# Layer 0: when GpSimd masks the adjacency tiles of x's side and of the late table

## The chip, the cores and the metric

The kernel runs on one core of a Trainium2 chip. The metric is the device time of the program in microseconds; the median of three runs before is 3467.49 us (3466.55 to 3467.74).

## The reference

Four graph layers run one after the other on x (64 x 256 x 256) with adjacency matrices adj (64 x 256 x 256), each with a residual sum and a layer norm. The change concerns layer 0, a recurrence over the 256 nodes: step i replaces row i of h, and later steps read it.

```python
d = jnp.sum(adj, axis=-1)
dinv = jnp.where(d != 0, 1.0 / jnp.where(d != 0, d, 1.0), 0.0)
norm_adjT = jnp.swapaxes(adj, 1, 2) * dinv[:, :, None]
def step(h, i):
    x = jnp.take(h_e, i, axis=1)
    row = jnp.take(norm_adjT, i, axis=1)
    x_par = jnp.einsum('bj,bjd->bd', row, h)
    iou = x @ W_ioux.T + b_ioux + x_par @ W_iouh.T + b_iouh
    r, z = jnp.split(iou, 2, axis=1)
    r, z = (jax.nn.sigmoid(r), jax.nn.sigmoid(z))
    hc = jnp.tanh(x @ W_coux.T + b_coux + x_par * r @ W_couh.T + b_couh)
    h_new = z * x_par + (1.0 - z) * hc
    return (jax.lax.dynamic_update_slice(h, h_new[:, None, :], (0, i, 0)), None)
h_out, _ = jax.lax.scan(step, h_e, jnp.arange(n))
```

x_par of node i is thus a sum over nodes not yet replaced (their h is still x) and over nodes already replaced (their h is new).

## The kernel before

Layer 0 is the loop over `now` in `_recurrence`, one turn for each node; the other layers follow. The order of the instructions on every engine is written out by hand (`manual_schedule`). Steps are grouped in parts of U = 8 and blocks of T = 32. Below, p is a step's place in its part (0 to 7), i its place in its block (0 to 31), k the block.

The sum x_par is gathered in tiles `ACC`, one for each part, from these sources:

- **x's side**: nodes that are not yet replaced. For the first 128 nodes it is computed before the loop; for the last 128 nodes the generator `x_side` (from L317) does it inside the loop, in sixteen tiles of XB = 4 batch entries. A tile is loaded in two transfers (`xA` from adj, `xX` from x; three buffers each), its `xA` is masked with a triangle by `cut` (L332, a multiplication on GpSimd, called POOL in the profile), and then four products run on PE (L212), one for each turn of the generator. Its results go through PSUM, ACT and DRAM (`Us`) into `ACC`.
- **near and far**: each new state is added to the next nodes at once, on DVE (`push`, L628) for the nearest, and on POOL (`push_far`, L661 and L665) for the rest of this part and the next.
- **late**: states between about one part and 64 steps back, added by PE (L519) for a part at a time, from a ring `Hw` of states and a masked table `An`; the result goes through DRAM (`Lb`, L499 and L505), and POOL adds it to `ACC` in steps with p = 5 and 6 (L874).
- **early**: older states, by products on PE (L416), through DRAM (`Es`); POOL adds them where p = 3 and 4 (L815).

Before a step ends, POOL multiplies the next node's sum by dinv into `ready` (L802); DVE uses it in v (L851), and v leads to the next x_par (`xp`, L865).

`fill_early` is called twice in a step with p of 4 to 7: once just ahead of the r gate's matmuls (h_part, L603), once just behind those of z. It runs an early product where one is due, and otherwise one turn of `x_side`, or two where p is 6 or 7. A turn's matmuls stand in PE's queue at that place, whatever they wait for.

In `x_side`, a tile counts as landed when both of its transfers were issued more than two steps ago (`landed`). With the last product of a tile the generator masks the next tile if that has landed; if not, it masks it in a later turn and uses up that turn.

`late_load(k + 1, n)` is called at i = 0 of block k. It asks for the table's raw rows (`raw`, one buffer, in two or four pieces, each in turn in the list of loads) and puts four masks of a quarter each (`cut`, L477, on POOL) at the end of given steps by `at_step`. A `cut` that finds a piece of raw not yet issued first issues loads from the list until all pieces are (`next_load`). Otherwise two loads are taken from the list at the end of each step with p below 4. All these transfers are issued by SP, in its order. The table is first read at i = 24.

In block k the degrees of block k + 1 are summed on DVE as a background task; its last piece, `inverse` (L226 to L230), comes at i = 22, at the end of a step.

Of the kernel before, what the change touches and what calls it, by code (L numbers as in the profile page):

```python
# [70 lines left out]
def _recurrence(tc, ident, Hd, x, adj, W_ioux, b_ioux, W_iouh, b_iouh, W_coux, b_coux, W_couh, b_couh, wide, then):  # L71
# [20 lines left out]
    B, N, D = x.shape  # L92
# [6 lines left out]
    XB = 4  # L99
    NG = B // 4  # L100
    HB = B // 2
    FAR = (2, 4, 4, 4, 4, 4, 3, 4)

    with ExitStack() as ctx:
# [13 lines left out]
        def ring(lo, hi):  # L118

            while lo < hi:  # L120
                end = min(hi, (lo // W + 1) * W)
                yield lo, end, lo % W
                lo = end
# [85 lines left out]
        def x_product(pb, at, A, Xs):  # L209

            for jc, (a, xs) in enumerate(zip(A, Xs)):
                nc.tensor.matmul(  # L212
                    pb[:, at, :], a, xs, start=(jc == 0), stop=(jc == len(A) - 1)
                )

        def x_out(half, b, ub):

            for c in range(2):
                nc.sync.dma_start(
                    Us[c, b:b + 4, half * P:(half + 1) * P, :].rearrange("b i f -> i b f"),  # L220
                    ub[:, :, c * P:(c + 1) * P],
                )
# [26 lines left out]
        def next_load(n):  # L249
            if loads:  # L250
                loads.pop(0)[1](n)

        def copy_later(out, in_, then=None):
            def f(n):
                nc.scalar.copy(out, in_)
                held.pop(0)
                if then:
                    then(n)

            copies.append(f)  # L260

        def load_later(out, in_, rank):

            begun = []

            def f(n):
                with nc.allow_non_contiguous_dma(reason="bias vector across partitions"):
                    nc.sync.dma_start(out, in_)
                begun.append(n)

            loads.append((rank, f))
            loads.sort(key=lambda e: e[0])
            return begun

        def landed(begun, n):

            return all(f and n > f[0] + 2 for f in begun)

        def at_step(n, f):
            transfers.setdefault(n, []).append(f)  # L280
# [3 lines left out]
        def base_bank(shape, name):  # L284

            while len(held) == 3:
                next_of(copies, now)
            held.append(name)
            return ps.tile(shape, F32, tag="base", name=name, bufs=3)
# [29 lines left out]
        ahead = []  # L319

        def x_side():

            def load(g):
                A = stream.tile([P, XB, P], F32, tag="xA", name=f"xA2_{g}", bufs=3)
                Xs = stream.tile([P, XB, D], F32, tag="xX", name=f"xX2_{g}", bufs=3)
                return A, Xs, [
                    load_later(to, of.rearrange("b j d -> j b d"), 2)
                    for to, of in ((A, adj[g:g + XB, P:N, P:N]), (Xs, x[g:g + XB, P:N, :]))
                ]

            def cut(A):
                nc.gpsimd.tensor_mul(A, A, tri.unsqueeze(1).to_broadcast([P, XB, P]))  # L332

            tiles = [load(e * XB) for e in range(3)]
            ahead = False
            n = yield
            for g in range(0, B, XB):
                A, Xs, last = tiles.pop(0)
                while not ahead:
                    if landed(last, n):  # L340
                        cut(A)
                        ahead = True
                    n = yield
                ub = stream.tile([P, 4, D], F32, tag="ub", name=f"xu2_{g}")
                for b in range(0, XB, 2):
                    pb = base_bank([P, 2, D], f"xp2_{g}_{b}")
                    for q in range(2):
                        x_product(pb, q, [A[:, b + q, :]], [Xs[:, b + q, :]])
                        if q:
                            copy_later(ub[:, b:b + 2, :], pb, None if b + 2 < XB else (  # L350
                                lambda n, b=g, ub=ub: at_step(n + 1, lambda: x_out(1, b, ub))
                            ))
                            if b + 2 == XB:
                                ahead = bool(tiles) and landed(tiles[0][2], n)
                                if ahead:
                                    cut(tiles[0][0])
                                if g + 3 * XB < B:
                                    tiles.append(load(g + 3 * XB))
                        n = yield


# [90 lines left out]
        def late_load(k, n=None):  # L452


            An = blk.tile([P, HB, U, T // U], F32, tag="An", name=f"An_{k}")
            raw = stream.tile([P, HB, T], F32, tag="raw", name=f"raw_{k}", bufs=1)
            first, last = k * T - W + T // 2, k * T + T // 2
            if first < 0:
                nc.gpsimd.memset(raw, 0.0)
            begun = []  # L460
            for lo, hi, at in ring(max(first, 0), last):
                for g in range(2):
                    to = raw[g * W + at:g * W + at + hi - lo]
                    of = adj[g * HB:(g + 1) * HB, lo:hi, k * T:(k + 1) * T].rearrange(
                        "b j i -> j b i"
                    )
                    if n is None:
                        nc.scalar.dma_start(to, of)
                    else:
                        begun.append(load_later(to, of, 1.5))  # L470

            def cut(lo):
                while not all(begun):
                    next_load(now)
                part = raw[:, lo:lo + HB // 4].rearrange("p b (s u) -> p b s u", u=U)
                take = window[k % 2].rearrange("p (s u) -> p s u", u=U).unsqueeze(1)
                nc.gpsimd.tensor_mul(  # L477
                    An[:, lo:lo + HB // 4].rearrange("p b u s -> p b s u"), part,
                    take.to_broadcast(list(part.shape)),
                )  # L480

            for e in range(4):
                if n is None:
                    cut(e * HB // 4)
                else:
                    at_step(n + 20 + e, lambda e=e: cut(e * HB // 4))
            return An

        def late(first):
# [188 lines left out]
        with tc.tile_pool(name="r_first_ps", bufs=4, space=bass.MemoryType.PSUM) as xps:  # L678
            for g in range(0, B, GB):
# [4 lines left out]
                for n in range(0, GB, 4):  # L684
                    ub = fst.tile([P, 4, D], F32, tag="ub", name=f"xu_{g}_{n}")
                    for e in range(0, 4, 2):
                        pb = xps.tile([P, 2, D], F32, tag="x", name=f"xp_{g}_{n}_{e}")
                        for q in range(2):
                            b = n + e + q
# [22 lines left out]

        tables[0]["Sd"] = chain_S(0)
        tables[0]["An"] = late_load(0)
        xq = {a: load_x(a) for a in range(2)}
        for a in range(3):
# [18 lines left out]
        late_side = background = None  # L735
        behind = []
        x_left = x_side()
        next(x_left)

# [16 lines left out]
        for now in range(N):  # L756
            n = now
# [136 lines left out]
            if k + 1 < NB:  # L894
                if i == 0:
                    background = degrees(k + 1)
                if i in (0, 2, 3, 8, 10, 11, 12, 15, 16, 17, 19, 20, 22, 24):
                    next(background, None)
                if i == 0:
                    tables[k + 1]["S"], double = load_S(k + 1, n)  # L900
                    at_step(n + 19, double)
                    tables[k + 1]["An"] = late_load(k + 1, n)
                if i == 28:
                    tables[k + 1]["Sd"] = chain_S(k + 1)
# [569 lines left out]
```

## Time and profile before

| What | us |
|---|---|
| median of three runs | 3467.49 |
| the profiled execution, its own time | 3469.95 |
| its span in the trace | 3468.2 |
| PE busy | 3243.9 (94%) |
| DVE busy | 2505.5 (72%) |
| ACT busy | 1883.5 (54%) |
| POOL busy | 1874.3 (54%) |
| sixteen masks of x's side on POOL (L332), 155 to 1,620 us | 20.3 |
| twenty-eight masks of the late table on POOL (L477), 155 to 1,620 us | 20.7 |

The first 140 us set up weights and the first half of x's side; the loop runs from about 142 to 1,560 us; the rest is layers 1 to 3. A share of busy time is a mean over these stages. In the profile PEld is the weight load of a matmul, SPq the issuing of transfers by SP, and the number in brackets at the end of a timeline's line is how long the engine was idle ahead of that instruction, and what ended it. A wait that names two engines, one after the arrow, says who ended it.

### The profile page before, as it was taken

The numbers are of one execution on the slowest core, as the hardware profiler recorded it, in microseconds if no ns is written. First come the engines' busy times: TensorE is split into PE (matmuls) and PEld (weight loads), VectorE is DVE, ScalarE is ACT, GpSimd is POOL, SyncE is SP. The second block draws the span as 40 slices with busy tenths as digits, with TensorE's granted clock in tenths as the row PEclk, the third lists the DMA queues.
The fourth block names the chain that finished last, engine by engine and source line by source line (L and its number), as shares of the span: only waits on it lengthen the run. The fifth ranks groups of instructions, "written<-read, shape, count | busy, mean of one in ns | idle before, by whom it ended". The sixth has DMA issues, their size and how long they took to land.

```text
span 3468.2 us, 80349 instructions
## 1 busy us (share of the span) xinstructions
PE 3243.9 (94%) x29350; PEld 2331.3 (67%) x29350; DVE 2505.5 (72%) x7061; ACT 1883.5 (54%) x5010; POOL 1874.3 (54%) x2165
## 2 busy tenths in 40 slices
PE   5699999899899898887999999999999999999997
PEld 4555555555555555555888888888888888888885
DVE  3376766766666777754888888887888887888885
ACT  0254545545444454444666666666666666666664
POOL 2366676766566777743444444444444444444443
PEclk8999999999999999997999999999999999999999
DMA  9755576687787575321111111111111111111100
GB/s 293 228 156 138 159 178 153 154 187 194 188 207 166 143 174 146 97 58 58 47 46 47 47 47 46 47 47 46 47 46 46 47 47 46 47 47 46 47 29 21
DMA packets 389348, 347.89 MB, mean 100 GB/s; under 512 B 107356, under 2 KB 355304, under 8 KB 383720
## 3 DMA queue, kind: packets, MB, share of 16 engines
q1 hardware_dynamic: 371256, 325.82, 35.0%
q10 hardware_dynamic: 17696, 16.91, 1.5%
q8 instruction: 235, 3.85, 0.5%
q14 instruction: 161, 1.32, 0.1%
HBM read 224.01 MB, written 99.61 MB: 93 GB/s over the span
## 4 chain that ended last, share of the span: by engine, by line
PE 73%; DVE 7%; DMA 7%; POOL 5%; issue 4%; ACT 3%; SPq 2%; ACTq 0%; DVEq 0%; POOLq 0%
PE mm L995 13%; PE rc L603 5%; PE s L1179 4%; PE rc L595 4%; PE mm_2f L995 3%; PE mm_3v L995 3%; PE mm_t L995 3%; PE late L519 3%; PE mm_3f L995 3%; PE mm_2v L995 3%; PE mm_g L995 3%; PE mm_2s L995 3%; DVE ACC L628 3%; PE o L1214 3%; PE mm_2w L995 3%
## 5 line engine op out<-in xcount | busy, mean ns | idle before, releaser
L628 DVE SCALAR_TENSOR_TENSOR ACC<-keep,S,ACC 128x128 f32<-128x128 f32 x1712 | 504.3, 345 | 189.9 <-ACT hs L646 172.4
L1191 POOL TENSOR_TENSOR p3s<-p 128x256 f32<-128x256 f32 x512 | 387.6, 788 | 366.5 <-ACT p L1189 366.0
L995 PE MATMUL mm<-xT,weights 128*128 128x256 f32 x2048 | 481.9, 383 | 2.9 <-ACT xT L1077 2.9
L995 PEld LDWEIGHTS mm<-xT,weights 128*128 128x128 f32 x2048 | 384.8, 190 | 79.4 <-issue 25.5
L1188 DVE TENSOR_TENSOR p<-s,neg 128x512 f32<-128x512 f32 x512 | 317.7, 683 | 114.3 <-PE s L1179 114.3
L665 POOL TENSOR_TENSOR ACC<-ACC,far 128x384 f32<-128x384 f32 (+1 forms) x313 | 372.6, 1190 | 24.5
L595 PE MATMUL rc<-WxT,xqT 128*64 128x256 f32 x2048 | 330.2, 401 | 4.2 <-ACT rc L836 1.2
L661 POOL TENSOR_TENSOR far<-hs,S 128x384 f32<-128x384 f32 (+1 forms) x313 | 304.9, 974 | 4.7
L802 POOL TENSOR_TENSOR ready<-ACC,dinv 128x128 f32<-128x128 f32 x255 | 102.3, 401 | 369.6 <-DVE ACC L628 369.4
L959 ACT ACTIVATE y<-y,shift,rstd 128x256 f32<-128x256 f32 x512 | 273.4, 599 | 48.0 <-DVE shift L957 43.8
L1189 ACT ACTIVATE p<-p 128x512 f32<-128x512 f32 x512 | 295.0, 627 | 2.1 <-DVE p L1188 1.6
L1102 ACT ACTIVATE qk<-mm,weights 128x256 f32<-128x256 f32 x256 | 107.5, 471 | 268.9 <-PE mm L995 268.9
L1091 POOL TENSOR_TENSOR y<-y,g 128x512 f32<-128x512 f32 x64 | 81.1, 1267 | 267.5 <-issue 267.5
L1228 DVE RECIPROCAL rT<-o 128x256 f32<-128x256 f32 x128 | 223.8, 1748 | 0.3 <-PE o L1205 0.2
L947 DVE BATCH_NORM_STATS2 st<-y 128x6 f32<-128x256 f32 x512 | 209.0, 408 | 13.4 <-POOL y L1091 12.7
L951 POOL TENSOR_TENSOR rstd<-rstd,mhalf 128x2 f32<-128x2 f32 x256 | 173.8, 697 | 82.5 <-DVE rstd L950 80.7
L612 ACT COPY xpT<-xpT_ps 128x128 f32<-128x128 f32 x256 | 68.4, 267 | 259.7 <-PE xpT_ps L610 259.7
L603 PE MATMUL rc<-WhT,xpT 128*64 128x128 f32 x2048 | 171.3, 289 | 29.1 <-ACT xpT L612 28.6
L1056 POOL TENSOR_TENSOR dis<-dis,mhalf 128x2 f32<-128x2 f32 x64 | 44.9, 702 | 277.3 <-DVE dis L1055 260.7
L603 PEld LDWEIGHTS rc<-WhT,xpT 128*64 128x64 f32 x2048 | 108.4, 138 | 119.9 <-ACT xpT L612 84.2
L212 PE MATMUL xp<-xX,xA 128*128 128x256 f32 x384 | 115.7, 446 | 59.3 <-POOL xA L681 32.6
L1154 ACT ACTIVATE qk<-mm,weights 128x256 f32<-128x256 f32 x256 | 107.5, 471 | 115.9 <-PE mm L995 115.9
(162 smaller groups left out, 7501.7 us busy)
## 6 DMA issues: line engine op xcount, KB each, us to landing
xX<-in_x_dram ACTq DMA_DIRECT2D x16, 1024.0 KB
Us<-xu SPq DMA_DIRECT2D x64, 256.0 KB
xq<-in_x_dram SPq DMA_DIRECT2D x64, 256.0 KB
ACC<-Us SPq DMA_DIRECT2D x32, 512.0 KB
Es<-eu SPq DMA_DIRECT2D x64, 256.0 KB
early_sb<-Es SPq DMA_DIRECT2D x32, 512.0 KB
xin<-in_x_dram SPq DMA_DIRECT2D x64, 256.0 KB
ad<-in_adj_dram SPq DMA_DIRECT2D x64, 256.0 KB
```

Of the source, the lines that this page charges most:

```text
L595: nc.tensor.matmul(G[o * B:(o + 1) * B], xqT[a, i // 2][:, i % 2, kc, h * B:(h + 1) * B], WxT[:, kc, o, gates], start=False, stop=False, s ...
L603: nc.tensor.matmul(G[o * B:(o + 1) * B], hT[:, kc * B:(kc + 1) * B], WhT[:, kc, o, g], start=False, stop=(kc == 1), skip_group_check=True,)
L628: nc.vector.scalar_tensor_tensor(acc[:, 0, :], keep[:, j % 2, :], s, acc[:, 0, :], ALU.mult, ALU.add)
L661: nc.gpsimd.tensor_mul(tmp[:, 0:count, :], hs.unsqueeze(1).to_broadcast(shape), s.unsqueeze(2).to_broadcast(shape),)
L665: nc.gpsimd.tensor_add(acc, acc, tmp[:, 0:count, :])
L947: nc.vector.bn_stats(st, y[:, c, :])
L959: nc.scalar.activation(y[:, c, :], y[:, c, :], AF.Identity, bias=shift[:, c:c + 1], scale=rstd[:, c:c + 1],)
L995: nc.tensor.matmul(pm[:, c, :], lhsT[:, k, c * P:(c + 1) * P], rhs[:, k, :], start=(k == 0), stop=(k == 1),)
L1188: nc.vector.tensor_add(p, s_ps[i], self.neg3)
L1189: nc.scalar.activation(p, p, AF.Exp, scale=ISQ)
L1191: nc.gpsimd.tensor_add(both, p[:, 0, :], p[:, 1, :])
L1228: nc.vector.reciprocal(rT, o_ps[:, 1, :])
```

## The change

In `x_side` a tile is masked after any product of the tile before, as soon as it has landed, and not only with the last one. The four masks of the late table are put at the ends of the steps with i = 12, 15, 20 and 23; before, they were at 20, 21, 22 and 23.

```diff
@@ x_side
                     n = yield
+                ahead = False
                 ub = stream.tile([P, 4, D], F32, tag="ub", name=f"xu2_{g}")
                 for b in range(0, XB, 2):
                     pb = base_bank([P, 2, D], f"xp2_{g}_{b}")
...
-                            if b + 2 == XB:
-                                ahead = bool(tiles) and landed(tiles[0][2], n)
-                                if ahead:
-                                    cut(tiles[0][0])
-                                if g + 3 * XB < B:
-                                    tiles.append(load(g + 3 * XB))
+                            if b + 2 == XB and g + 3 * XB < B:
+                                tiles.append(load(g + 3 * XB))
+                        if not ahead and tiles and landed(tiles[0][2], n):
+
+                            cut(tiles[0][0])
+                            ahead = True
                         n = yield
@@ late_load
-                    at_step(n + 20 + e, lambda e=e: cut(e * HB // 4))
+                    at_step(n + (12, 15, 20, 23)[e], lambda e=e: cut(e * HB // 4))
```

## The prediction

> **What bounds the kernel now.** The page came first: it tells that two stretches follow one another, a recurrence of 256 steps up to about 1,555 us and layers 1 to 3 after it, in which PE is busy 99% of the time (1649.28 of 1669.00 us in the table of windows). Only the recurrence can gain. Its chain hops between engines:
>
> ```profile
> PE 73%; DVE 7%; DMA 7%; POOL 5%; issue 4%; ACT 3%; SPq 2%; ACTq 0%; DVEq 0%; POOLq 0%
> ```
>
> Next I read who waited for whom from 155 to 600 us, the stretch with the sixteen masks of L332 (1.27 us each on POOL):
>
> ```profile
> POOL ready L802 <- DVE ACC L628: 134.5, 66, 5.9
> PEld xp L212 <- POOL xA L332: 16.5, 7, 3.0
> ```
>
> Columns are the total, the times and the longest. POOL has about 2 us of idle before a typical `ready`, so it isn't short of time; yet PE stands 16.5 us in seven waits for masks. (The table repeats 13.7 us of the same waits for PE's matmul side; they are not added.) The chain of waits shows one of the seven at step 31:
>
> ```profile
> 311.79 0.40 POOL ready L802
> 312.19 1.00 POOL far L661
> ...
> 313.27 1.26 POOL ACC L665
> 314.53 1.23 POOL xA L332
> ...
> 315.81 0.91 PE xp L212 x2
> 316.72 0.21 PE rT_ps L610
> 316.93 1.05 PE rc L595 x4
> 317.98 0.85 PE rc L603 x8
> ```
>
> The mask was put into POOL's queue with the last product of the tile before, hence behind `ready` and `far`; the next product stood ahead of the step's own matmuls in PE's queue. These then ran slowly: L595 x4 takes 0.65 us elsewhere, here 1.05. The table of windows says why (four stretches; PEclk is the third figure from the end of a line, ahead of the DMA share and GB/s):
>
> ```profile
> 216.04:219.44 3.40, 3.40 (x29) 2.26 (x31) 1.63 (x6) 1.40 (x6) 3.17 (x4) 1.00 0.14 43
> 316.20:319.60 3.40, 3.40 (x19) 1.74 (x17) 0.39 (x2) 1.47 (x4) 0.00 (x0) 0.50 0.00 0
> 398.80:402.20 3.40, 3.36 (x31) 2.15 (x32) 0.93 (x3) 1.52 (x4) 1.21 (x1) 1.00 0.11 33
> 442.50:445.90 3.40, 3.40 (x21) 2.62 (x17) 1.56 (x5) 0.99 (x4) 2.85 (x4) 0.50 0.02 7
> ```
>
> After five of the seven waits (261.6, 316.2, 442.5, 497.1, 582.4) PE has half its clock for 3.4 us; after those at 216 and 398.8 it has not. A step's length is the distance between the r sigmoids (L826) in ACT's timeline; here steps 31 and 32:
>
> ```profile
> 312.29 0.26 ACT L826 ACTIVATE rc<-rc 128x128 f32<-128x128 f32 x1 [1.03 <-PE rc L603]
> ...
> 321.88 0.26 ACT L826 ACTIVATE rc<-rc 128x128 f32<-128x128 f32 x1
> ...
> 327.30 0.26 ACT L826 ACTIVATE rc<-rc 128x128 f32<-128x128 f32 x1 [0.76 <-PE rc L603]
> ```
>
> 9.6 us against 5.4.
>
> For the second edit I read An's masks (L477, 0.74 us each) against the timelines of DVE, SP and POOL, one line of each:
>
> ```profile
> 1176.80 0.65 DVE L227 TENSOR_TENSOR deg<-deg,deg 128x16 f32<-128x16 f32 x1
> ...
> 778.02 1.06 SPq L268 DMA_DIRECT2D raw<-in_adj_dram  x1
> ...
> 752.80 1.27 POOL L874 TENSOR_TENSOR ACC<-ACC,late_sb 128x512 f32<-128x512 f32 x1 [2.52 <-DMA late_sb<-Lb]
> ```
>
> L227 takes 0.17 us at 448.37, where POOL is idle, but 0.65 beside an An mask (1176.70 to 1177.43). raw's last piece is issued at step 113. The 752.80 line is one of ten waits of POOL for late_sb, 40.0 us in all: from 620 to 1,060 us a DMA chain limits many steps.
>
> **What the Trainium skill says.** "TensorE: Matmul & The Clock Gate", What's actually happening: the clock gate halves the PE clock after an idle window of about 3.4 us and restores it after a busy one; windows run free of the kernel, so the same gap may or may not cost a window. The trace agrees: slots of 3.4 us at 0.50, after some gaps only. "SBUF — State Buffer", Who interferes with whom: a DVE instruction with two SBUF inputs contends with a GpSimd instruction that reads SBUF, and a `tensor_scalar` can too; the loser blocks. L227's 0.65 for 0.17 agrees. "DMA: Bandwidth & Descriptors", Queues, rings and completion order: on one engine descriptors are consumed in ring order. Our packets agree in kind: raw's last piece for k=5 is issued at 976.25 and the An mask behind it starts at 984.32.
>
> **The change part by part.** The instructions are the same; only POOL's order moves, and two raw issues on SP. A half step is the distance between the two calls of `fill_early` in one step, or from one step's second to the next one's first.
>
> *Masks of xA.* Nine of sixteen move: tiles 12, 24, 32, 44, 56 by one to three steps, tiles 16, 36, 48, 60 by half a step. All seven waits belong to moved masks (before: steps 13, 21, 31, 46, 53, 63, 78). In the new order each mask has at least one half step, some 2.5 us, ahead of its product, so I take all waits as gone. What is late next is PE's own work: a step with four products but no wait. Such steps measured 5.26 (5, 45, 77), 5.35 (15), 5.26 (23). Old lengths: 13: 6.59; 21 and 22: 7.86, 6.18; 31: 9.59; 46: 7.85; 53 and 54: 7.61, 6.89; 63: 9.51; 78: 9.37; sum 71.45. New, estimated: 5.3; 5.3, 5.6; 5.4; 5.4; 5.3, 6.0 (eight products in series stay); 5.4; 5.4; sum 49.1. Gain **22.3 us**. Cross-check: 16.5 of waiting plus five slots at about 1.2 (up to half of 3.4 each) is 22.5.
>
> *The room for the moved masks.* Idle ahead of `ready` where they go: 2.79 (step 13), 2.87 (step 29), 0.86 (step 53), 0.77 (step 46). 1.27 fits the first two, and hangs over by about 0.4 in the last kind; v (L851), which uses `ready`, follows it by more than a microsecond in most steps. The masks of tiles 32 and 56 also come near the Sd product of step 28 of a block (DVE, two SBUF inputs), which may be blocked up to 1.27, and An's first mask joins two early adds in step 204. Together **+2** (0 to 4). SP issued the loads of tiles 32 and 56 at 286.68 and 467.91, some 9 us before their new places; packets of 512 B ended by 290 and 471, so no mask waits for its tile.
>
> *An, steps 21 and 22 relieved.* In blocks 2, 3, 5 and 6 L227 falls back from 0.65 or 0.59 to 0.17: 4 x 0.47 = **-1.9**. At 1179.7 and 1350.4 a half-clock slot follows (steps 183 and 215 take 7.0 and 7.1, not 5.3). Beyond the 0.47 that leaves 1.2 each; a shorter gap may or may not avoid it, so 0 to -2.4, taken **-1.2**. In block 4 the chain has An itself (0.69 at 991.95), L227 of 1.20 and L229 of 0.41; An's first mask there held `ready` until 985.01, and raw's 1,536 packets of 13 ns over 16 engines, 1.3 us, lie ahead of Lb: **-3** (-1 to -4).
>
> *An, steps 12 and 15.* A mask costs 0.74; step 20 carries the same load today at 5.7 to 5.8 against 5.7 for step 12, so the work is free. The wait isn't, in two blocks: raw_4 and raw_5 have a piece that SP issued only at steps 113 and 147; the cut at step 12 of the block (108, 140) now forces it out ahead of late_sb's issue. Behind the mask stand `ready`, far and the late add, and DVE's v waits for `ready`. Step 108: SP is free at 747.87 and idle till 749.21; 512 packets, landing about 750.7 by late_sb's 3.46 us less its size (estimate); mask to 751.5, `ready` 751.5 instead of 747.52, v 3 us late, of which 1 is slack; the 2.52 wait for late_sb swallows what follows: **+2** (0 to 6). Step 140: issue about 937.4, landing about 941, `ready` 941.7 instead of 932.99, so step 141 stalls where 142 stalled (7.45 us for late_sb at 943.20), late_sb comes about 1.9 later; sigma(142) at 946.5 and xp at 949.7 instead of 945.83: **+3.9** (0 to 8). For the upper end I use the 8 us of 976.25 to 984.32. The other blocks' raw packets end before the cut (556 to 558 against 570; 1,113 against 1,124; 1,287 against 1,295).
>
> *Given back to DMA.* The DMA engines are 63% busy from 300 to 600 us; steps that come sooner meet transfers that don't. I take a tenth of the gain, **+2** (0 to 8).
>
> Sum: -22.3 + 2 - 1.9 - 1.2 - 3 + 2 + 3.9 + 2 = **-18.5 us**. The profiled execution took 3469.95 (span 3468.2), the median 3467.49; a difference passes unchanged to either: 3449.0.
>
> **Rivals.** (a) More: all displacement hidden, both slots of 183 and 215 gone, raw free: -22.3 - 1.9 - 2.4 - 4 = -30.6, near 3437. For it: POOL's idle. Against: a wait that must precede `ready` at 140. (b) Little: the DMA chain takes 8 us back, raw costs 6 and 8, displacement 4, relief only 2: -22.3 + 26 - 2 = +1.7, about 3467 and anywhere within 7. For it: late_sb waits already limit those blocks. Against: there are hardly any before 600 us, where the gain lies. (c) Slower: the wait for raw at step 12. If its last piece came 8 us late in all six blocks, with the half clock after each stall (1.7), it would cost 6 x 9.7 = 58 less the existing late_sb waits there, about 20: +38 - 26 = +12, 3479. It decides from 27 us in all, 4.5 per block; the packets show four blocks landing in time, which speaks against. (d) The masks don't move: excluded by the order of POOL's queue, 1%.
>
> **How the numbers follow.** Forecast (about 3449, own range 3442 to 3458): 0.77. (a) 0.09, (b) 0.08, (c) 0.05, (d) 0.01. For 8 in 10 I take 3440 to 3460. What can be told from no change is 0.2%, 6.9 us: faster means below 3460.6. Forecast and (a) give 0.86; half of (b), (d) and a little make 0.07 the same; the rest slower, 0.07.
>
> **What would show it.** PE's wait for L332 falls from 16.5 us to under 2; no half-clock slot stands near 261, 316, 442, 497 or 582 less the shift; steps 31 and 63 measure about 5.4; L227 0.17. A POOL gap on DMA raw stands ahead of An at steps 108 and 140. The prediction is wrong if xp still waits for xA, or if raw's waits exceed 8 us each.

## The result and the profile after

The changed kernel takes 3439.05 us (median of four runs, 3437.49 to 3443.41) against 3467.02 (3466.18 to 3467.74): 0.9924 of the time before, 95% interval 0.9908 to 0.9941, 28 us less. In a second comparison (the fifth experiment) the ratio was 0.9921 (0.9903 to 0.9940). The direction and the place were forecast; the size was not: 18.5 us were expected, and the median lies 0.95 us below the low end of the range.

The span of the profiled execution fell from 3468.2 to 3437.6 us. The page of the changed kernel, its first line and its chain:

```profile
span 3437.6 us, 80347 instructions
...
PE 73%; DMA 7%; DVE 7%; POOL 4%; issue 3%; ACT 3%; SPq 2%; ACTq 0%; DVEq 0%; POOLq 0%
```

POOL lost a hundredth of the chain. Who waited for whom, 155 to 600 us of the changed kernel (total, times, longest):

```profile
POOL ready L803 <- DVE ACC L629: 112.9, 64, 4.2
...
POOL ACC L875 <- DMA late_sb<-Lb: 5.8, 3, 3.3
```

The lines of PE that waited for L332, 16.5 us in all before, are gone from this answer: PE no longer waits for a mask of xA. (Behind the edit all lines of the file are one further on: L803 is what was L802.) The waits for late_sb in this window grew from 1.8 to 5.8 us.

Step 31 in the chain of the changed kernel, and the sigmoids of steps 31 and 32 in ACT's timeline:

```profile
307.30 0.44 PE z_ps L604 x8
307.73 1.06 PE xp L212 x4
308.80 0.11 PE rT_ps L611
308.90 0.58 PE rc L596 x4
309.49 0.49 PE rc L604 x8
```

```profile
307.40 0.26 ACT L827 ACTIVATE rc<-rc 128x128 f32<-128x128 f32 x1 [1.03 <-PE rc L604]
312.60 0.26 ACT L827 ACTIVATE rc<-rc 128x128 f32<-128x128 f32 x1
```

The step takes 5.2 us, not 9.6. The same four matmuls (L212 x4) now follow the z gate at once, and what comes after them runs at the usual pace. The reason stands in POOL's timeline: the mask of tile 32 was done three steps before.

```profile
292.84 1.27 POOL L666 TENSOR_TENSOR ACC<-ACC,far 128x512 f32<-128x512 f32 x1
294.07 1.27 POOL L332 TENSOR_TENSOR xA<-xA,tri 128x512 f32<-128x512 f32 x1
297.00 0.40 POOL L803 TENSOR_TENSOR ready<-ACC,dinv 128x128 f32<-128x128 f32 x1 [1.65 <-DVE ACC L629]
```

It filled idle time: 1.65 us of idle is still left ahead of `ready`. And the granted clock stays whole (PEclk, third from the end) where it was halved:

```profile
305.50:308.90 3.40, 3.40 (x30) 2.48 (x30) 2.19 (x8) 1.43 (x6) 2.43 (x4) 1.00 0.24 71
427.00:430.40 3.40, 3.40 (x34) 2.62 (x33) 2.38 (x9) 1.28 (x6) 3.32 (x5) 1.00 0.16 48
```

Where did the time come from? This table is worked out from the starts of the r sigmoids of steps 0, 96, 160 and 255, for every profiled execution of the study; the rest is the setup ahead of step 0 and the layers behind. Each line is one execution. That of before took 3469.95 us, more than the median of before in any comparison, so differences from its line come out 3 to 12 us larger than the comparisons of many runs below.

```
                      steps 0-96   96-160   160-255
before                   534.2      378.4    500.1
changed                  510.4      376.8    493.4
e1 x side alone          511.6      378.4    499.2
e2 An alone              528.3      378.3    494.2
e3 An at 20,20,23,23     513.7      377.1    497.2
e4 one quarter moved     531.6      379.6    496.2
e5 changed, again        513.4      374.2    495.0
e6 raw issued sooner     511.6      382.5    495.8
e7 PE kept busy          530.2      371.7    502.0
e8 xA not masked         513.4      376.1    500.9
e9 fewer transfers       511.6      367.4    496.6
```

Between before and changed the columns fall by 23.8, 1.6 and 6.7 us. The first follows the masks of xA: it is 510.4 to 513.7 in the seven executions where they come early or are left out, and 528.3 to 534.2 in the other four. The third follows An's masks: 493.4 to 497.2 where none stands at step 22 of a block, 499.2 to 502.0 where one does. The middle (blocks 3 and 4) shows no such order. In e1, e7 and e8 its code is that of before, and these four took 371.7 to 378.4, so a few us between two executions prove nothing there.

In the middle a new wait did appear. POOL and SP at step 109 in the changed kernel, from their timelines:

```profile
719.70 1.27 POOL L816 TENSOR_TENSOR ACC<-ACC,early_sb 128x512 f32<-128x512 f32 x1
727.37 0.73 POOL L478 TENSOR_TENSOR An<-raw,window 128x256 f32<-128x256 f32 x1 [6.40 <-DMA raw<-in_adj_dram]
728.05 0.40 POOL L803 TENSOR_TENSOR ready<-ACC,dinv 128x128 f32<-128x128 f32 x1
```

```profile
723.59 0.45 SPq L268 DMA_DIRECT2D raw<-in_adj_dram  x1
724.34 0.34 SPq L506 DMA_DIRECT2D late_sb<-Lb  x1
```

An waits 6.40 us for raw, which SP issued at 723.59; 9.29 us at step 141. Step 109 grows from 5.0 to 9.8, step 141 from 5.0 to 12.7. But step 112 falls from 10.2 to 5.4 and 142 from 10.7 to 5.8: steps 109 to 112 together cost 1.2 us more, 141 to 144 1.0 more. This holds for the first stall in the other executions too: with step 108, these steps take 30.3 to 32.6 us in the six that leave raw where it was and 29.6 to 33.0 in the three with the changed masks of An and the transfers of before (changed, e2, e5). The second stall costs more than this pair shows: steps 141 to 144 take 25.7 to 27.8 us in the six, with a mean of 26.7, and 28.3 to 30.2 in the three, with a mean of 29.1.

In the timeline of DVE at step 182, L227 has its short form again:

```profile
1148.44 0.17 DVE L226 TENSOR_SCALAR deg<-deg 128x16 f32<-128x16 f32 x1
1148.65 0.17 DVE L227 TENSOR_TENSOR deg<-deg,deg 128x16 f32<-128x16 f32 x1
```

Steps 183 and 215 take 5.3 us, not 7.0 and 7.1.

### The profile page after: what moved, and what is told of

It reads as the page before. It is cut to its first block, busy times and chain, and to the rows that moved or that the text cites. A ratio compares the mean times of both kernels' runs of the same rounds, so it can differ in the third digit from the quotient of the medians.

```text
span 3437.6 us, 80347 instructions
## 1 busy us (share of the span) xinstructions
PE 3227.2 (94%) x29350; PEld 2321.8 (68%) x29350; DVE 2499.7 (73%) x7061; ACT 1883.7 (55%) x5010; POOL 1873.5 (55%) x2165
## 4 chain that ended last, share of the span: by engine, by line
PE 73%; DMA 7%; DVE 7%; POOL 4%; issue 3%; ACT 3%; SPq 2%; ACTq 0%; DVEq 0%; POOLq 0%
PE mm L996 13%; PE rc L604 5%; PE s L1180 4%; PE rc L596 4%; PE mm_2f L996 3%; PE mm_3v L996 3%; PE mm_t L996 3%; PE mm_3f L996 3%; PE mm_2v L996 3%; PE mm_g L996 3%; PE mm_2s L996 3%; PE mm_2w L996 3%; PE o L1215 3%; PE late L520 3%; DVE ACC L629 3%
## 5 line engine op out<-in xcount | busy, mean ns | idle before, releaser
L803 POOL TENSOR_TENSOR ready<-ACC,dinv 128x128 f32<-128x128 f32 x255 | 102.3, 401 | 335.3 <-DVE ACC L629 335.2
L948 DVE BATCH_NORM_STATS2 st<-y 128x6 f32<-128x256 f32 x512 | 209.0, 408 | 13.5 <-POOL y L1092 12.7
L604 PE MATMUL rc<-WhT,xpT 128*64 128x128 f32 x2048 | 170.2, 288 | 29.1 <-ACT xpT L613 28.9
L596 PE MATMUL z_ps<-WxT,xqT 128*64 128x128 f32 x2048 | 169.7, 287 | 0.0
```

The lines of the kernel that those rows point to most:

```text
L596: nc.tensor.matmul(G[o * B:(o + 1) * B], xqT[a, i // 2][:, i % 2, kc, h * B:(h + 1) * B], WxT[:, kc, o, gates], start=False, stop=False, s ...
L604: nc.tensor.matmul(G[o * B:(o + 1) * B], hT[:, kc * B:(kc + 1) * B], WhT[:, kc, o, g], start=False, stop=(kc == 1), skip_group_check=True,)
L948: nc.vector.bn_stats(st, y[:, c, :])
```

## The experiments

Each was timed against the kernel before in rounds on the same chip; 0.1% is 3.5 us.

**First: the x side alone.**

```diff
-                    at_step(n + (12, 15, 20, 23)[e], lambda e=e: cut(e * HB // 4))
+                    at_step(n + 20 + e, lambda e=e: cut(e * HB // 4))
```

> The x side's masks early, An's masks left at steps 20 to 23 of a block. Theory 'masks': the gain of the change lies in the seven waits for L332 and the half-clock slots behind five of them. Blocks 0 to 2 came out 23.8 us shorter in the changed kernel, so this kernel takes about 3467.0 - 23.8 = 3443 us; steps 31 and 63 measure about 5.2, and step 150 stays near 9. Rival 'given back': the DMA chain of blocks 3 and 4 takes part of it back once An's masks stand where they stood: 3450 to 3455, with waits for late_sb longer than 40 us in all.

Measured: 0.9941 (0.9926 to 0.9957), 20.3 us less than before; no wait for L332, steps 31 and 63 at 5.2 us, step 150 at 9.0. Steps 0 to 96 gave 22.6 us, the other stretches 0.0 and 0.9. The waits for late_sb come to 41 us, as before. 'Masks' holds; the median of 3444.85 lies between the two figures, and 'given back' finds no sign in the stretches.

**Second: An's masks alone.**

```diff
-                    at_step(n + 20 + e, lambda e=e: cut(e * HB // 4))
+                    at_step(n + (12, 15, 20, 23)[e], lambda e=e: cut(e * HB // 4))
```

> An's masks at steps 12, 15, 20, 23, the x side as before. Theory 'swallowed': raw's wait at steps 109 and 141 only takes the place of later DMA stalls (steps 112 and 142), net +1 to +2 each block, while step 22 relieved of An gives 2.2 in each of blocks 5 and 6 and some in 2 to 4: 3460 to 3464 us. Rival 'raw costs what it lasts': the steps 109 and 141 longer by 4.8 and 7.7 with nothing back: 12.5 less about 8 of relief, 3469 to 3473 us.

Measured: 0.9986 (0.9978 to 0.9994), 4.9 us less, within the figures of 'swallowed'. Step 109 grew to 9.5 and 141 to 13.2, while 112 fell to 5.4 and 142 to 6.7; the last stretch gave 5.9. One thing wasn't foreseen: in this execution steps 21, 22, 53, 54 and 63 were also shorter by 0.8 to 1.3 each, although PE still had seven waits for L332; three of the half-clock slots of before (262, 442, 497) were absent. The chain of before shows a reason at step 21:

```profile
259.15 0.69 POOL An L477
259.84 1.23 POOL xA L332
```

An's mask stood directly ahead of xA's, there and at step 53. With it moved away, PE's waits at these two places fell from 2.15 and 2.16 us to 1.46, and no half-clock slot followed. Steps 21, 22, 53 and 54 gave 4.6 us in this profile. In the changed kernel the first edit gives this relief already, so An's part isn't quite independent of x's, and 'swallowed', which didn't know of it, met its figures in part by luck. At 497 the wait was even longer (3.70 us, not 2.96) and the slot was absent all the same; why is open.

**Third: An's masks in pairs, at 20, 20, 23 and 23,** with the x side as changed.

```diff
-                    at_step(n + (12, 15, 20, 23)[e], lambda e=e: cut(e * HB // 4))
+                    at_step(n + (20, 20, 23, 23)[e], lambda e=e: cut(e * HB // 4))
```

> As the changed kernel, but An's four masks at steps 20, 20, 23, 23, so that steps 21 and 22 are free of them and raw isn't forced out at step 12. Theory 'swallowed': steps 109 and 141 fall back to 5.0, the old stalls at 112 and 142 return: 3436 to 3440 us. Rival 'raw costs what it lasts': 12.5 us less than the changed kernel, about 3427. Rival 'pairs block POOL': two masks in a row (1.48 us) hold up ready at steps 21 and 24 by up to 0.7 in six blocks: 3441 to 3446.

Measured: 0.9936 (0.9923 to 0.9949). POOL doesn't wait for raw; steps 109 and 141 are back at 5.0, and 142 at 10.5. Step 112 came back only to 6.6, but 158 took 13.1 instead of 6.8. The stretch of steps 96 to 160 took 377.1 us against 376.8: if it is the same stall, it had only changed its place. 'Raw costs what it lasts' (3427 us) falls. The median of 3443.83 lies in the figures of 'pairs block POOL', but of the steps with two masks at their end only some of those with i = 23 grew against the changed kernel (55, 119, 183, 215), by 0.3 to 0.5, so that reason isn't shown for the whole; by the interval this kernel can't be told from the changed one.

**Fourth: one quarter of An moved from step 22 to 23,** in the kernel before.

```diff
-                    at_step(n + 20 + e, lambda e=e: cut(e * HB // 4))
+                    at_step(n + (20, 21, 23, 23)[e], lambda e=e: cut(e * HB // 4))
```

> The kernel before with one thing moved: the third quarter of An's masks from step 22 to step 23 (20, 21, 23, 23). Theory 'port and clock': L227 falls from 0.65 to 0.17 us in blocks 2 to 6 and the half-clock slots of steps 183 and 215 go; those two steps fall from 7.0 to about 5.3, blocks 2 and 3 gain 0.5 each, block 4 1 to 2: 3461 to 3463 us. Rival 'clock stays': only 0.47 us for each of five blocks, about 3464.7, steps 183 and 215 near 6.5.

Measured: 0.9997 (0.9989 to 1.0005), not to be told from before. The timeline of DVE shows L227 relieved all the same:

```profile
1169.82 0.46 DVE L226 TENSOR_SCALAR deg<-deg 128x16 f32<-128x16 f32 x1
1170.31 0.17 DVE L227 TENSOR_TENSOR deg<-deg,deg 128x16 f32<-128x16 f32 x1
```

L227 is at 0.17 (not in block 4, where the late add still runs beside it: 1.19), the half-clock slots of steps 183 and 215 are gone, and each of these takes 5.55. So in the steps that it named, the first theory holds for L227 and for the clock; in blocks 2, 3, 5 and 6 the two steps at this place are 4.7 us shorter together. That it shows in the time, by 4 to 6 us, was wrong: the interval ends at 3.8 us less, and the runs scatter from 3459.5 to 3470.3. The eighth experiment parts the two effects. There An's mask is back at step 22 and L227 takes 0.65 us again, but no slot follows, and steps 183 and 215 take 5.60. So most of the 1.8 us at each of these steps is the slot, which comes after some such delays and not after others.

**Fifth: the changed kernel again.**

> The changed kernel itself once more, on the chip of the runs beside it, so that they can be compared with it. Theory 'parts add': the x part alone measured 0.9941 of before, An's part alone 0.9986, so together 0.9927. Rival 'An's part only helps while the x side waits': no better than the x part alone, 0.994.

Measured: 0.9921 (0.9903 to 0.9940). The two parts' product is 0.9927: they add, as far as these intervals tell. The rival's 0.994 is the upper end of the interval and isn't excluded. It is right for the relief of steps 21 and 53, which exists only while the x side waits, but not for steps 183 and 215, which are shorter here too (5.26 and 5.25 us).

**Sixth: raw's last piece issued ahead of Lb.**

```diff
-                for _ in range(2):
+                for _ in range(3 if n in (107, 139) else 2):
                     next_load(n)
```

> The changed kernel with one more load taken from the list at steps 107 and 139, so that raw's last piece is issued ahead of Lb and not behind it (two issues on SP move, nothing else). POOL's wait for raw at steps 109 and 141 (6.4 and 9.3 us) should shrink to under 3. Theory 'conserved': blocks 3 and 4 last as long as their DMA queue needs; the stall only moves to late_sb or Hw in later steps, steps 96 to 159 together within 3 us of the changed kernel, the time within 0.1%. Rival 'raw costs what it lasts': 10 to 12 us less than the changed kernel.

Measured: 0.9936 (0.9919 to 0.9953), 382.5 us for steps 96 to 160. POOL's wait for raw fell to 2.06 us at step 109, but only to 6.98 at step 141: the expectation of under 3 missed there. SP's timeline, and POOL's behind it:

```profile
710.80 10.41 SPq L268 DMA_DIRECT2D raw<-in_adj_dram  x3
721.31 1.89 SPq L500 DMA_DIRECT2D Lb<-lb  x2
...
725.72 0.35 SPq L506 DMA_DIRECT2D late_sb<-Lb  x1
```

```profile
723.50 0.74 POOL L478 TENSOR_TENSOR An<-raw,window 128x256 f32<-128x256 f32 x1 [2.06 <-DMA raw<-in_adj_dram]
...
731.83 1.26 POOL L875 TENSOR_TENSOR ACC<-ACC,late_sb 128x512 f32<-128x512 f32 x1 [4.89 <-DMA late_sb<-Lb]
```

SP is held 10.41 us in issuing three pieces, so the issue of Lb runs from 721.31 to 723.20; in the changed kernel it ran from 714.78 to 721.17. What An no longer waits at step 109, the late add waits at step 110. 'Conserved' holds for the total as far as the intervals tell, with 5.7 us in the stretch where 3 were allowed, in the losing direction; the gain of 10 to 12 us is refuted.

**Seventh: PE kept busy in the waits,** in the kernel before.

```diff
+                        if b + q == 0 and g in (24, 32, 44, 56, 60):
+                            for e in range(3):
+                                x_product(pb, q, [ident], [Xs[:, e, :]])
                         x_product(pb, q, [A[:, b + q, :]], [Xs[:, b + q, :]])
```

> The kernel before, with three more products (six matmuls, about 2.3 us, their result overwritten) ahead of the first product of tiles 24, 32, 44, 56 and 60, where PE otherwise waits for the mask. The waits for L332 stay, PE is busy in them. Theory 'wait and clock': in the x part alone, waits without a half-clock slot gave back 3.6 us for 3.9 us of waiting, those with one 19.8 for 12.6, thus 1.4 a slot; without the five slots (262, 316, 443, 497, 582) this kernel takes about 7 us less than before, and steps 31, 63, 78 fall by 1.4 each. Rival 'the slots cost nothing of their own': no change, or longer by some 2 us of added matmuls.

Measured: 0.9977 (0.9969 to 0.9985), 8.0 us less, with thirty matmuls more. The table of windows, at the places of the old slots:

```profile
313.90:317.30 3.40, 3.10 (x30) 1.90 (x31) 0.82 (x3) 1.52 (x4) 0.24 (x1) 1.00 0.10 20
439.00:442.40 3.40, 3.40 (x29) 2.27 (x31) 1.47 (x5) 1.44 (x6) 3.17 (x4) 1.00 0.08 23
```

All five slots are gone. PE still waits for the masks, 10.7 us by the list of waits, where the added matmuls don't cover it; steps 31 and 78 fall by 1.6 and 1.5, 21 and 22 by 1.6 together, 53 and 54 by 1.7, 63 by only 0.8: 7.1 in all, and the interval of the runs is 5.2 to 10.8. The fourth experiment gives the same measure without an added matmul: at step 31 PE waits 2.95 us there, as before, but no slot follows, and the step takes 8.01 us instead of 9.59. The clock is thus a cost of its own beside the wait, about 7 of the masks' 23 us. That the added matmuls alone kept away all five slots isn't shown by one profile, as slots were absent in others too.

**Eighth: xA not masked inside the loop,** An's masks at 20 to 23. The products take the tiles without the triangle.

```diff
-                nc.gpsimd.tensor_mul(A, A, tri.unsqueeze(1).to_broadcast([P, XB, P]))
+                pass
```

> The x part alone (An's masks at 20 to 23) with the sixteen masks of xA inside the loop left out: the products take the unmasked tiles. Theory 'free': masks placed early lie in POOL's idle time, so the time is that of the x part alone (0.994 of before) within 0.1%. Rival 'displaced': moved masks still push ready in steps 13, 29, 46, 53 and others, the 2 us of the prediction's sum; then this kernel is 2 to 4 us faster than the x part alone.

Measured: 0.9939 (0.9925 to 0.9954) against 0.9941 with the masks. 'Free' holds: sixteen masks of 1.27 us, 20 us of POOL, cost no measurable time where they stand now. By the runs alone 2 us couldn't be told (each interval reaches 5 us to either side), but the steps of 'displaced' can be compared one by one: 13, 29, 46 and 53 last the same with and without masks, to 0.01 us.

**Ninth: fewer transfers in blocks 3 and 4.**

```diff
+                if r == 0 or k not in (4, 5):
                     rows = stream.tile([P, R, N], F32, tag="rows", name=f"rows_{k}_{r}", bufs=1)
                     for h in range(2):
```

> The changed kernel, but in blocks 3 and 4 (the degrees of blocks 4 and 5) only the first of four loads of rows is made and summed four times, so those degrees are not the reference's; 1.5 MB of transfers fall out of each of the two blocks, nothing else. Steps 96 to 160 took 374 to 378 us in the changed kernel and within 372 to 383 in every variant. Theory 'the DMA queue sets blocks 3 and 4': 3 MB at the 195 GB/s of that stretch are 15 us; these steps fall by 8 to 16 us, POOL's waits for raw and late_sb with them. Rival 'latency': each stall is the round trip of Lb and late_sb, which the load doesn't change: under 3 us less.

Measured: 0.9921 (0.9893 to 0.9948). Steps 96 to 160 took 367.4 us, the shortest of all, 7 to 9 less than in the two executions of the changed kernel; the expectation was 8 to 16. POOL's waits for raw fell to 2.3 and 6.7 us, but those for late_sb at steps 126 and 134 grew to 8.1 and 7.9. Whether the load of the queue counts stays open. Four executions with the same code in these steps lay 6.7 us apart, this one is the fastest of its four runs (3430.50 to 3442.53), the DMA engines were busy 79% of 700 to 1,040 us against 81%, and the ratio can't tell this kernel from the changed one. What sets the stalls at 126 and 134 stays open.

## Why the prediction was right in kind and short in size

- **Masks of xA, -22.3:** right. The nine steps fell from 71.45 to 48.12, by 23.3. All seven waits went, with the five half-clock slots; the split of 16.5 us of waiting and about 1.2 a slot agrees with the 7.1 us of the seventh experiment. The runs of the first experiment give 20.3 us for the x side, where this term and the two charges of 2 come to 18.3.
- **Room for the moved masks, +2:** wrong, it is nothing in the steps that I named. The eighth experiment shows them alike with masks and without. The idle ahead of `ready` was a better guide than the overhang of 0.4 us that I added for four places.
- **Given back to DMA, +2:** not shown either way. In this pair it didn't come: the other 87 steps up to 96 took 462.3 after 462.8, although the waits for late_sb grew from 1.8 to 5.8 us. But in the other six executions with early masks or none they took 463.0 to 465.6, and 461.8 to 465.8 in the other three with late ones.
- **An, blocks 2, 3, 5 and 6, -1.9, and the two slots, -1.2:** right in kind and too small; L227 is at 0.17 us as said, and both slots went, so the lower bound of -2.4 was nearer there. With the steps before them, 182, 183, 214 and 215 gave 4.4 us, where these two terms had 2.1 for blocks 5 and 6. A further 3.1 us of the last stretch came from step 163, a stall that took anything from 5.5 to 9.6 us from execution to execution: that is luck.
- **An, block 4, -3:** right in size where it was expected. Steps 149 and 150 fell from 15.0 to 11.7 us; they take 10.7 to 12.4 in the other four executions with the changed masks of An and 14.1 to 15.1 in those with the old ones. One of its reasons was wrong: L227 of block 4 still takes 1.20 us, beside the late add.
- **Raw, +2 and +3.9:** this is the step that was furthest off. The waits were about as long as I reckoned (6.40 and 9.29 us; from the ends of the early adds at 745.95 and 931.43 to my landings it was 4.8 and 9.6), yet in this pair they cost 1.2 and 1.0 us. I followed each stall for one step and stopped there: step 112's stall of 4.8 us went, and after 142's, 143 and 144 were 1.8 us shorter too. By the executions compared above it was about 0.5 and 2.4, so the swallowing is clear for the first stall and only in part for the second. The sum for blocks 3 and 4 was +2.4 and measured -1.6 in this pair, but this stretch as a whole scatters too much to decide between the two.
- **Rivals:** the case 'more' (3437, 0.09) came nearest, but raw wasn't free, as it assumed, and block 4 gave about 3 us, not 4. 'Slower' rested on raw's wait; it took place in two blocks, as the packets had told, and was mostly swallowed.

In this pair the masks' 1.0 us, the room's 2, the 2.3 of blocks 5 and 6 and the 3.7 of raw add up to 9.0 of the 9.5 us between forecast and median. That this comes out so well is partly luck, as other steps changed by as much between executions. Costs that I charged to be careful are the larger part of it.

## What to carry to other kernels

A filler instruction in an engine's queue that waits for a helper engine blocks all that stands behind it; issue the helper's part as soon as its data is there, into idle time; here it then cost nothing that the steps show. A wait of 2 to 3 us on PE can cost more through the clock (here about 7 us beside 16.5 of waiting), so count the slots at half clock beside the waits. Where a stretch is bound by a chain of transfers, charge a new wait there only with what it adds to the chain: a stall that comes sooner can take the place of the next one (here 5.9 us were charged and 2 to 3 came). And before you read a few us from one stretch, compare executions whose code is the same there.

## What the runs showed of the hardware

Waits of 1.46 and 2.40 us were followed by no half-clock slot, others of 2.15 and 2.16 us by one of 3.4 us. A wait of 2.96 us at step 31 had a slot before, one of 2.95 in the fourth experiment had none, and one of 3.70 in the second had none: the length of the gap alone does not decide it. With thirty added matmuls in those gaps the kernel was 8.0 us faster (5.2 to 10.8). A DVE `tensor_tensor` on 16 elements a partition took up to 1.2 us beside GpSimd's work and 0.17 us alone. SP was held 10.41 us by issuing three transfers, of which the first took 0.59 us and the others 4.43 and 5.30; what held it isn't shown.
